# First layer of a two-layer kernel: the value product as seven half-size products, and the output product in another place of the period

## The chip, the cores and the metric

The kernel runs on one core of a Trainium2 chip. A core has a matrix engine (PE, TensorE), a vector engine (DVE), an activation engine (ACT), a general engine (POOL, GpSimd) and a queue that only issues transfers here (SP, SyncE). Each engine has its own stream of instructions and carries them out in program order; semaphores order the streams against one another. Tiles live in SBUF; matmul results go to PSUM, which has eight banks of 128 partitions x 512 fp32 values.

The metric is device time of one execution in microseconds (us). The kernel before takes 935.56 us, the median of three runs (935.55 to 936.3).

## The reference

Eight batches of 512 tokens with 256 features pass through two layers. In both, the layer's input is normalised and two branches are added to it.

```python
scores = einsum('bnqd,bnkd->bnqk', q, k) / sqrt(L)          # q, k: xn @ W + b, then RoPE; 16 heads of L=64
attn   = softmax(where(causal, scores, -1e9))
attended = einsum('bnqk,bnkd->bnqd', attn, v)               # v = xn @ Wv + bv
x = x + attended @ Wo + bo + quantised(xn)                  # int8 rounding of xn, product with int8 weights
xn = layernorm(x)
x = x + (mask * softmax(comparison)) @ xn + sigmoid(xr @ Wr.T) * (square(relu(xk @ Wk.T)) @ Wv2.T)
```

`RoPE` multiplies by cosines and sines, with the sines meeting the other member of each pair. The scale of the quantised branch is the greatest magnitude over all eight batches, so that branch can only begin when the last batch has been normalised. The second layer isn't touched by the change.

## The kernel before

All products of the attention are fp32. The first layer works on 16 groups, `at` = 0 to 15: group `at` is batch `b = at // 2` and half `g = at % 2` of its 16 heads, 8 heads each. The order of all instructions is written out by hand (`tc.manual_schedule()`); no planner decides it, and each engine's stream follows from the order of the calls. The loop at L842, `for at in range(1, last)` with `last = 15`, handles in one period several groups at different stages: it ends group `at-1`, does the softmax of group `at`, and projects for groups `at+1` and `at+2`.

The matrix engine's order in one period is: scores of run 0 (L509); the weighing product of group `at-1`, probabilities times values (`weigh`, L597); scores of run 1; the queries' product for group `at+1` (`project(at+1, 0)`, L428); scores of run 2; the values' product for group `at+1` (`project_v`, L472); scores of runs 3 and 4; the output product of group `at-1` (`finish`, which calls `output_product`, L390, and `add_output`, L399, for each half); the keys' product for group `at+2` (`project(at+2, 1)`, L428). The scores of a group are cut by query blocks into five runs (`RUNS`, L34), so that softmax on the other engines can follow run by run.

A `project` call for a group of 8 heads is two calls of `project_qk` (indices `2*at` and `2*at+1`, four heads each). In one, two products go into two banks; ACT moves each to a tile `l` with its bias (L434); four DMAs on SP copy `l` to a tile `y` with its quarters of partitions exchanged (L436). `turn_qk` then does the RoPE: DVE multiplies `h = l * cos` (`turn_own`, L446) and `y = y * sin` (`turn_other`, L446), and POOL adds them (`h = h + y`, L461). The `l` and `y` tiles have two buffers each.

`project_v` makes the values of a group in four banks, each from four matmuls of 512 columns (two per bank for each of the two halves of the 256 input features), which ACT copies to a tile `v` (L478); two DMAs store it to DRAM (`va<-v`, L479), and `load_v` fetches it in another layout (`vr<-va`, L489) after the next period's weighing.

`soften` is the lower part, in which DVE reads the scores from PSUM, adds the mask, scales and finds the row minimum of the negated scores (L537), and then the exponential on ACT, with its sum (L541). `divide` takes reciprocals on DVE (L552) and multiplies by them on POOL (L560). `turn` transposes the probabilities on DVE (L580). The probabilities lie in a pool, `prob`, with four buffers for each tag (a tag is a kind of tile).

The next batches' input is handled in the same loop: `look_at` (statistics), `prepare` (normalising, greatest magnitude), `turn_x` (DVE transposes in L325, SP stores the result with `xnf<-xs`, L329, and fetches it as `xnT` with four DMAs, `xnT<-xnf`, L188), and `load_x` for the batch after it (L81). `look_at` and `prepare` come in odd periods, `turn_x` and `load_x` in even ones from `at = 4`; batches up to 2 are turned on PE (`transpose_x`). SP takes all its transfers in program order, and waits at each for what it needs; the four fetches of `xnT` wait until the store of the same data has landed.

`add_biases` (L380) adds the output bias to a batch's result on POOL. In periods 12 and 13 the first two batches' quantised products are fitted in (`fetch_input`, `round_input`, `clip`, `add_quantised`). `bank` gives the eight banks of PSUM in rotation. A bank asked for again waits until its last reader is done.

## Time and profile before

| what | value |
|---|---|
| median of three runs | 935.56 us (935.55 to 936.3) |
| profiled execution, span | 934.3 us |
| profiled execution's own time | not listed apart; the median is 1.3 us above the span, for what lies around it |
| granted clock of the matrix engine | 1.00 in every period looked at |
| length of periods 7, 8, 9 and 10 (between starts of weighing) | 44.24, 44.51, 44.23, 45.70 us |
| length of periods 1, 12, 13, 14 | 45.50, 45.97, 44.92, 42.73 us |
| value product (L472), 256 matmuls in all | 114.3 us |
| output product (L390), 512 matmuls in all | 114.9 us |

The profile is of one execution. For each engine it lists busy time and idle time, and what ended the idle time (the releaser). Matmuls are pipelined, so the length of a single matmul says less than that of a run of equal ones: 16 of 512 columns are 7.06 us from first to next, 32 of 256 columns 7.10 us. The busy time that a group shows can be more than such a row gives for each instruction, as neighbours overlap. The chain of work is followed back from the last instruction, at each step to what released it. Tile names are `out<-in`; `sc` are scores, `pq` the queries' or keys' bank, `pv` the values' bank, `pw` the output product's bank, `av` the weighed values, `p` the probabilities, `t` their transposes.

### The profile page before, as it was taken

What the parts mean: (1) busy time and instruction counts of PE and PEld (TensorE: products, weight loads), DVE (VectorE), ACT (ScalarE), POOL (GpSimd) and SP (SyncE); (2) the same over time, 40 slices, a digit from 0 to 9 for tenths busy, and PEclk for the clock granted to TensorE, in tenths of its full rate; (3) what the DMA queues carried; (4) which work ended last, traced back from release to release, by engine and by line L of the source; (5) the groups of instructions that cost most, each with busy time, mean ns of one, the idle gap of its engine ahead of it and who ended that gap; (6) DMA issues with size and microseconds to landing.
All of it is one profiled execution on the core that took longest, in us unless ns stands there. A gap on an engine that the chain in (4) does not pass through costs nothing.

```text
span 934.3 us, 27432 instructions
## 1 busy us (share of the span) xinstructions
PE 919.8 (98%) x10451; PEld 594.7 (64%) x10451; DVE 793.3 (85%) x2441; ACT 528.3 (57%) x1478; POOL 542.2 (58%) x688
## 2 busy tenths in 40 slices
PE   9998999999999999999999999999999999999998
PEld 5446565656566575757565656566657777777776
DVE  4998898898899889988998899999899588888854
ACT  3585564647465646474746556555577444445553
POOL 2576766655665667566665756678667323444311
PEclk9999999999999999999999999999999999999999
DMA  7667354525543464245444635563435133221011
GB/s 213 194 165 213 102 138 130 121 75 132 169 105 97 109 182 132 75 115 172 123 95 114 179 93 145 151 154 97 110 108 127 47 102 79 74 50 48 25 33 34
DMA packets 70290, 108.03 MB, mean 116 GB/s; under 512 B 8592, under 2 KB 49040, under 8 KB 70160
## 3 DMA queue, kind: packets, MB, share of 16 engines
q1 hardware_dynamic: 68288, 104.64, 42.2%
q10 hardware_dynamic: 1872, 1.64, 0.7%
q8 instruction: 83, 1.36, 0.6%
q14 instruction: 47, 0.39, 0.1%
HBM read 41.76 MB, written 28.84 MB: 76 GB/s over the span
## 4 chain that ended last, share of the span: by engine, by line
PE 85%; DVE 6%; DMA 3%; issue 1%; POOL 1%; SPq 1%; ACT 1%; DVEq 0%; ACTq 0%; POOLq 0%
PE pq L428 21%; PE av L597 14%; PE sc L509 11%; PE pw L390 10%; PE pv L472 8%; PE po L756 6%; PE pk L703 3%; PE pg L718 3%; PE pvv L730 3%; DVE t L580 2%; PE c L675 2%; PE trc L743 1%; PE plr L245 1%; DVE p L537 1%; DMA xnl<-xnf 1%
## 5 line engine op out<-in xcount | busy, mean ns | idle before, releaser
L541 ACT ACTIVATE p<-p,nm 128x64 f32<-128x64 f32 (+15 forms) x512 | 260.0, 512 | 123.8 <-DVE nm L537 100.9
L560 POOL TENSOR_SCALAR p<-p,rs 128x512 f32<-128x512 f32 (+4 forms) x504 | 265.4, 547 | 44.6 <-DVE rs L552 42.6
L461 POOL TENSOR_TENSOR h<-h,y 128x1024 f32<-128x1024 f32 x62 | 161.1, 2598 | 181.5 <-DVE y L446 102.2
L537 DVE CUSTOM_DVE_ANT_0 p<-sc,cmask 128x64 f32<-128x64 f32 (+15 forms) x512 | 190.2, 434 | 53.7 <-PE sc L509 53.7
L580 DVE STREAM_TRANSPOSE t<-p 128x256 f32<-128x256 f32 (+3 forms) x640 | 192.2, 367 | 17.9 <-POOL p L560 17.8
L509 PE MATMUL sc<-h,h 64*32 64x512 f32 (+15 forms) x4096 | 138.7, 393 | 1.3 <-POOL h L461 1.2
L597 PE MATMUL av<-t,vr 32*64 32x384 f32 (+15 forms) x4096 | 128.8, 392 | 3.7 <-issue 3.7
L597 PEld LDWEIGHTS av<-t,vr 32*64 32x64 f32 x4096 | 122.8, 131 | 9.2 <-issue 7.9
L509 PEld LDWEIGHTS sc<-h,h 64*32 64x32 f32 x4096 | 78.6, 106 | 78.5 <-issue 58.3
L434 ACT ACTIVATE l<-pq,cs 128x512 f32<-128x512 f32 x128 | 84.7, 683 | 67.6 <-PE pq L428 53.3
L390 PE MATMUL pw<-wo,att 128*128 128x256 f32 x512 | 114.9, 382 | 0.8 <-DVE nm L537 0.8
L446 DVE TENSOR_TENSOR y<-y,cs 128x1024 f32<-128x1024 f32 x64 | 110.6, 1728 | 5.1 <-DMA y<-l 5.1
L428 PE MATMUL pq<-xnT,wq 128*128 128x512 f32 x256 | 114.6, 599 | 0.2 <-ACT xnT L349 0.2
L428 PE MATMUL pq<-xnT,wk 128*128 128x512 f32 x256 | 113.1, 593 | 1.4 <-DVE x L399 1.0
L472 PE MATMUL pv<-wv,xnT 128*128 128x512 f32 x256 | 114.3, 599 | 0.0
L390 PEld LDWEIGHTS pw<-wo,att 128*128 128x128 f32 x512 | 95.9, 190 | 19.5 <-issue 6.1
L541 ACT ACTIVATION_READ_ACCUMULATOR p<-p,nm 128x1 f32 x512 | 97.3, 190 | 0.0
L428 PEld LDWEIGHTS pq<-xnT,wk 128*128 128x128 f32 x256 | 48.3, 190 | 58.2 <-issue 55.4
L472 PEld LDWEIGHTS pv<-wv,xnT 128*128 128x128 f32 x256 | 47.3, 190 | 57.9 <-issue 54.5
L446 DVE TENSOR_TENSOR h<-l,cs 128x1024 f32<-128x1024 f32 x64 | 80.0, 1252 | 4.3 <-ACT l L434 4.3
L428 PEld LDWEIGHTS pq<-xnT,wq 128*128 128x128 f32 x256 | 47.2, 190 | 56.0 <-issue 48.8
L611 ACT ACTIVATE att<-av,cs 128x512 f32<-128x512 f32 x64 | 38.7, 688 | 71.3 <-PE av L597 71.3
(114 smaller groups left out, 940.7 us busy)
## 6 DMA issues: line engine op xcount, KB each, us to landing
y<-l SPq DMA_DIRECT2D x256, 128.0 KB, 2.3
va<-v SPq DMA_DIRECT2D x32, 512.0 KB, 3.1
vr<-va SPq DMA_DIRECT2D x64, 256.0 KB, 5.1
x<-in_x SPq DMA_DIRECT2D x15, 512.0 KB, 5.0
x1f<-x SPq DMA_DIRECT2D x7, 512.0 KB, 3.2
out<-y SPq DMA_DIRECT2D x14, 256.0 KB, 2.2
xnf<-xs SPq DMA_DIRECT2D x5, 512.0 KB, 3.6
xnT<-xnf SPq DMA_DIRECT2D x20, 128.0 KB, 2.8
```

The costliest lines, as they stand in the source:

```text
L390: nc.tensor.matmul(pw[:, j, :], atts[at, p][:, tok], wo[:, 4 * (at % NH) + p, :], start=(p == 0), stop=(p == 3),)
L428: nc.tensor.matmul(pb.rearrange("p (t a r) -> p t a r", a=4, r=Q), w[:, g, k, bass.ts(t, P)], xnT[b][:, k].rearrange("p a (t r) -> p t a r ...
L434: nc.scalar.activation(l[:, t, :], pb, AF.Identity, bias=cs[:, bias : bias + 1])
L446: nc.vector.tensor_tensor(dst, src, table[:, None, :].to_broadcast([P, 2, S]), ALU.mult)
L461: (engine or nc.gpsimd).tensor_tensor(h, h, y, ALU.add)
L472: nc.tensor.matmul(pb.rearrange("p (g n) -> p g n", g=2), xnT[b][:, k, 2 * half + j], wqkv[2][:, 2 * g : 2 * g + 2, k, :], start=(k == 0), ...
L509: nc.tensor.matmul(scored[at, i][e][j * Q : j * Q + Q, :], q[rows, j % 2, bass.ts(i, Q)], k[rows, j % 2, :n], start=True, stop=True,)
L537: nc.vector.tensor_tensor_reduce(p[:, e, col : col + n], sc, cmask[:, S - n :], -1.0 / L**0.5, BIG, ALU.add, ALU.min, nm[:, c : c + 1],)
L541: nc.scalar.activation(p[:, e, col : col + n], p[:, e, col : col + n], AF.Exp, bias=nm[:, c : c + 1], scale=-1.0, accum_out=sm[:, c : c + 1],)
L560: nc.gpsimd.tensor_scalar(p, p, rs[:, c : c + 1], 1.0, ALU.mult, ALU.mult)
L580: nc.vector.transpose(turned[at][c][:, :, at_ : at_ + (n - 1) * pitch(c) + 1 : pitch(c), :], p[:, :, c * P : c * P + n * Q].rearrange("p e ...
L597: nc.tensor.matmul(banks[j][e * L : e * L + L, i * Q :], vs[at][rows, c, m, bass.ts(e, L)], t[c][rows, e, m * pitch(c) + m : m * pitch(c) ...
```

## The change

The value product of groups 2 to 15 is made by `project_v_by_seven`. The product is seen as two by two blocks: the 256 input features in two halves, the token tiles in two halves on one side, and the weight columns of the group in two halves on the other. With sums and differences of blocks (the Winograd form of Strassen's scheme) seven block products give what eight gave. Each is two matmuls of 256 columns, so 28 matmuls instead of 16 of 512. Four of them go to one bank, `x`, one after another: each adds to what is there, and ACT copies the bank after each (`keep`). One goes to bank `y` and two to bank `z`; DVE adds those banks to the kept copies (`add`), three times. The sums of weight blocks are made once, on POOL, at `at = 1` (`sum_weights`, four operations, which overwrite a block of `wv`); the differences of input blocks are made on POOL once for each batch, in odd periods (`mix_input`, four operations).

The order of the period changes with it. `finish(at-1)`, the output product, comes between runs 2 and 3 of the scores, where `project_v` was. `project_v_by_seven(at+1)` ends the period. The keys' product for the first four heads of `at+2` comes before it; that for the other four is cut in two, one bank after the second product into `x` and one after the third, by way of `amid`, which also holds the exponential and division of run 4 and the transposes of runs 3 and 4. `soften` is cut into `lower` and `raise_`. `turn_own` and `turn_other` of the second queries stand around the division of run 3.

`look_at(b+2)` comes before the scores of run 1 and `prepare(b+2)` before the division of run 1, instead of after the scores of run 1 and after the division of run 2. `turn_x(b+1)` and `load_x(b+2)` come before the division of run 1 and the queries' product in periods 4, 6, 8 and 10, instead of after the division of run 2; in period 12 `turn_x(7)` comes ahead of the division of run 2. In period 14 the seven products have nothing between them, and the loop is left after them.

The pool of probabilities has six buffers, and the program is built with `dynamic_dma_scratch_size=1024`.

```diff
--- before
+++ after
@@ -267,3 +267,3 @@
         qk = pool("qk", 4)
-        prob = pool("prob", 4)
+        prob = pool("prob", 6)
         attp = pool("att", 4)
@@ -383,6 +383,8 @@
 
-        def output_product(at, half):
+        def output_product(at, half, js=(0, 1)):
 
-            pw = bank(f"pw_{at}_{half}").rearrange("p (j n) -> p j n", j=2)
-            for j in range(2):
+            if 0 in js:
+                products[at, half] = bank(f"pw_{at}_{half}").rearrange("p (j n) -> p j n", j=2)
+            pw = products[at, half]
+            for j in js:
                 tok = bass.ts(2 * half + j, P)
@@ -393,3 +395,2 @@
                     )
-            products[at, half] = pw
 
@@ -414,3 +415,3 @@
 
-        def project_qk(at, which):
+        def project_qk(at, which, ts=(0, 1)):
 
@@ -420,7 +421,10 @@
 
-            l, y = (
-                prob.tile([P, 2, S], F32, tag="p", name=f"{tag}_{at}_{which}") if at == 1 else
-                work.tile([P, 2, S], F32, tag=tag, name=f"{tag}_{at}_{which}", bufs=2) for tag in "ly"
-            )
-            for t in range(2):
+            if 0 in ts:
+                evicted[at, which] = [
+                    prob.tile([P, 2, S], F32, tag="p", name=f"{tag}_{at}_{which}") if at == 1 else
+                    work.tile([P, 2, S], F32, tag=tag, name=f"{tag}_{at}_{which}", bufs=2)
+                    for tag in "ly"
+                ]
+            l, y = evicted[at, which]
+            for t in ts:
                 pb = bank(f"pq_{at}_{which}_{t}")
@@ -434,5 +438,5 @@
                 nc.scalar.activation(l[:, t, :], pb, AF.Identity, bias=cs[:, bias : bias + 1])
-            for n in range(4):
-                nc.sync.dma_start(y[bass.ts(n ^ 1, Q)], l[bass.ts(n, Q)])
-            evicted[at, which] = l, y
+            if 1 in ts:
+                for n in range(4):
+                    nc.sync.dma_start(y[bass.ts(n ^ 1, Q)], l[bass.ts(n, Q)])
 
@@ -483,2 +487,82 @@
 
+        wv = wqkv[2].rearrange("p (g h) k n -> p g h k n", h=2)
+        wv_sums = work.tile([P, 2, 3, 2 * P], F32, name="wv_sums")
+
+        def sum_weights():
+            one, two, three = (wv_sums[:, :, n] for n in range(3))
+            (a11, a12), (a21, a22) = ([wv[:, :, h, k] for k in range(NK)] for h in range(2))
+            for dst, x, y, op in (
+                (one, a21, a22, ALU.add), (two, one, a11, ALU.subtract),
+                (a21, a11, a21, ALU.subtract), (three, a12, two, ALU.subtract),
+            ):
+                nc.gpsimd.tensor_tensor(dst, x, y, op)
+
+        mixes = {}
+
+        def mix_input(b):
+            t = work.tile([P, 4, 2, P], F32, tag="tx", name=f"tx_{b}")
+            (b11, b12), (b21, b22) = ([xnT[b][:, k, 2 * h : 2 * h + 2] for h in range(2)] for k in range(NK))
+            for dst, x, y in ((0, b12, b11), (1, b22, t[:, 0]), (2, b22, b12), (3, b21, t[:, 1])):
+                nc.gpsimd.tensor_tensor(t[:, dst], x, y, ALU.subtract)
+            mixes[b] = t
+
+        def project_v_by_seven(at, amid={}):
+            b, g = divmod(at, NH)
+            stores[at] = away.tile([4, P, NT * P], F32, tag="v", name=f"va_{at}")
+            s1, s2, s4 = (wv_sums[:, g, n] for n in range(3))
+            (a11, a12), (s3, a22) = ([wv[:, g, h, k] for k in range(NK)] for h in range(2))
+            t1, t2, t3, t4 = (mixes[b][:, n] for n in range(4))
+            b11, b21, b22 = xnT[b][:, 0, 0:2], xnT[b][:, 1, 0:2], xnT[b][:, 1, 2:4]
+            x, y, z = (bank(f"pv_{at}_{n}").rearrange("p (j n) -> p j n", j=2) for n in range(3))
+            v = [work.tile([P, 4, 2, P], F32, tag="v", name=f"v_{at}_{half}", bufs=2) for half in range(2)]
+
+            def product(to, left, right, fresh=False):
+                for j in range(2):
+                    nc.tensor.matmul(
+                        to[:, j, :], left[:, j], right, start=fresh and j == 0, stop=True,
+                        skip_group_check=j > 0 or not fresh,
+                    )
+
+            def part(half, g_):
+                return v[half][:, 2 * g_ : 2 * g_ + 2].rearrange("p r j n -> p j r n")
+
+            def of(bank_):
+                return bank_.rearrange("p j (r n) -> p j r n", r=2)
+
+            def keep(half, g_):
+                nc.scalar.copy(part(half, g_), of(x))
+
+            def add(bank_, half, g_):
+                nc.vector.tensor_tensor(part(half, g_), of(bank_), part(half, g_), ALU.add)
+
+            def store(half):
+                nc.sync.dma_start(
+                    stores[at][:, :, half * 2 * P : half * 2 * P + 2 * P].rearrange("r p n -> p r n"),
+                    v[half].rearrange("p r t n -> p r (t n)"),
+                )
+
+            def then(step):
+                amid.get(step, lambda: None)()
+
+            product(x, b11, a11, True)
+            keep(0, 0)
+            then(0)
+            product(y, b21, a12, True)
+            product(z, t1, s1, True)
+            product(x, t2, s2)
+            keep(1, 0)
+            add(y, 0, 0)
+            then(1)
+            product(x, t3, s3)
+            keep(1, 1)
+            then(2)
+            add(z, 1, 1)
+            product(x, t4, a22)
+            keep(0, 1)
+            store(0)
+            then(3)
+            product(z, b22, s4)
+            add(z, 1, 0)
+            store(1)
+
         def load_v(at):
@@ -516,2 +600,6 @@
         def soften(at, run):
+            lower(at, run)
+            raise_(at, run)
+
+        def lower(at, run):
 
@@ -540,7 +628,15 @@
                         )
+                    col += n
+
+        def raise_(at, run):
+            nm, sm = sums_of[at][:2]
+            for us in RUNS[run]:
+                for i in us:
+                    for e in range(2):
+                        p = chances[at, i][:, e, :]
+                        c = 2 * PLACE[i] + e
                         nc.scalar.activation(
-                            p[:, e, col : col + n], p[:, e, col : col + n], AF.Exp,
-                            bias=nm[:, c : c + 1], scale=-1.0, accum_out=sm[:, c : c + 1],
+                            p, p, AF.Exp, bias=nm[:, c : c + 1], scale=-1.0,
+                            accum_out=sm[:, c : c + 1],
                         )
-                    col += n
 
@@ -567,3 +663,3 @@
 
-        def turn(at, run):
+        def turn(at, run, units=slice(None)):
 
@@ -574,3 +670,3 @@
                 ]
-            for i in (i for us in RUNS[run] for i in us):
+            for i in (i for us in RUNS[run][units] for i in us):
                 p = chances.pop((at, i))
@@ -847,3 +943,4 @@
             scores(at, 0)
-            turn(at - 1, 4)
+            if at == 1:
+                turn(at - 1, 4)
             soften(at, 0)
@@ -865,2 +962,4 @@
             turn_qk(2 * at + 3, 1)
+            if g == 1 and 1 <= b < B - 2:
+                look_at(b + 2)
             if at == last - 2:
@@ -876,3 +975,6 @@
             elif g == 1 and 1 <= b < B - 2:
-                look_at(b + 2)
+                prepare(b + 2)
+            if g == 0 and 1 < b < B - 2:
+                turn_x(b + 1)
+                x_next.append(load_x(b + 2))
             divide(at, 1)
@@ -881,2 +983,6 @@
             project(at + 1, 0)
+            if at == 1:
+                sum_weights()
+            if g == 1:
+                mix_input(b + 1)
             if at in (last - 3, last - 2):
@@ -890,2 +996,4 @@
                 clip(xnl, xq)
+            if at == last - 3:
+                turn_x(b + 1)
             divide(at, 2)
@@ -893,8 +1001,2 @@
                 prepare(2)
-            elif g == 1 and 1 <= b < B - 2:
-                prepare(b + 2)
-            if g == 0 and 1 < b < B - 1:
-                turn_x(b + 1)
-                if b + 2 < B:
-                    x_next.append(load_x(b + 2))
             if at == last - 1:
@@ -904,5 +1006,6 @@
                 add_biases(0)
-            project_v(at + 1)
             if at == last - 1:
+                project_v_by_seven(at + 1)
                 break
+            finish(at - 1)
             if at == 2:
@@ -911,8 +1014,6 @@
             scores(at, 3)
-            soften(at, 3)
-            turn_qk(2 * at + 3, 0)
-            turn(at, 2)
-            divide(at, 3)
+            lower(at, 3)
+            raise_(at, 3)
             scores(at, 4)
-            soften(at, 4)
+            lower(at, 4)
             if at in (last - 3, last - 2):
@@ -920,7 +1021,24 @@
                     add_quantised(s_, half, xq, line(f"u_{s_}_{half}"))
-            finish(at - 1)
-            turn(at, 3)
-            if two:
-                project(at + 2, 1)
-            divide(at, 4)
+            turn_own(2 * at + 3, 0)
+            divide(at, 3)
+            turn_other(2 * at + 3, 0)
+            project_qk(2 * at + 4, 1)
+            turn(at, 2)
+
+            def step_one():
+                raise_(at, 4)
+                divide(at, 4)
+
+            def step_two():
+                turn(at, 3, slice(0, 1))
+                project_qk(2 * at + 5, 1, (0,))
+
+            def step_last():
+                turn(at, 3, slice(1, 2))
+                turn(at, 4)
+
+            project_v_by_seven(
+                at + 1,
+                {0: step_one, 1: step_two, 2: lambda: project_qk(2 * at + 5, 1, (1,)), 3: step_last},
+            )
             if g == 0 and b < B - 1:
@@ -1096,3 +1214,5 @@
 
-    nc = bacc.Bacc("TRN2", target_bir_lowering=False, num_devices=1)
+    nc = bacc.Bacc(
+        "TRN2", target_bir_lowering=False, num_devices=1, dynamic_dma_scratch_size=1024
+    )
     arrays, args = {}, []
```

## The prediction, made before the result was known

> **What bounds the kernel now.** I read the busy times and the chain of work that ended last first.
>
> ```profile
> PE 919.8 (98%) x10451; PEld 594.7 (64%) x10451; DVE 793.3 (85%) x2441; ACT 528.3 (57%) x1478; POOL 542.2 (58%) x688
> ...
> PE 85%; DVE 6%; DMA 3%; issue 1%; POOL 1%; SPq 1%; ACT 1%; DVEq 0%; ACTq 0%; POOLq 0%
> PE pq L428 21%; PE av L597 14%; PE sc L509 11%; PE pw L390 10%; PE pv L472 8%; PE po L756 6%; PE pk L703 3%; PE pg L718 3%; PE pvv L730 3%; DVE t L580 2%; PE c L675 2%; PE trc L743 1%; PE plr L245 1%; DVE p L537 1%; DMA xnl<-xnf 1%
> ```
>
> TensorE (PE) is the bound, at 98% of the span; the value product (pv, L472) is 8% of the chain. So work taken off PE is time won, if the others keep up. VectorE (DVE), at 85%, is next. I cut the span at the starts of the weighing products (L597): one stretch is one period. Columns: stretch and length; then busy time and instructions of PE, weight loads, DVE, ACT, POOL; clock, DMA share, GB/s. The rows are periods 7, 8 and 10.
>
> ```profile
> 344.82:389.06 44.24, 44.24 (x595) 27.69 (x597) 41.15 (x138) 26.17 (x80) 27.62 (x37) 1.00 0.38 97
> 389.06:433.57 44.51, 44.51 (x595) 27.75 (x597) 37.77 (x128) 26.40 (x80) 29.14 (x40) 1.00 0.56 156
> 477.80:523.50 45.70, 45.01 (x595) 27.58 (x597) 37.76 (x128) 26.40 (x80) 29.12 (x40) 1.00 0.57 151
> ```
>
> PE is full in both kinds of period; an odd one leaves DVE 3.1 us free, an even one 6.7. Then period 8 engine by engine: PE, SyncE's queue (SP, which issues the DMAs in program order), DVE (start, length, line, tile).
>
> ```profile
> 399.25 7.13 PE L428 MATMUL pq<-xnT,wq 128*128 128x512 f32 x16
> 406.32 2.01 PE L509 MATMUL sc<-h,h 64*32 64x384 f32 x64
> 408.26 7.13 PE L472 MATMUL pv<-wv,xnT 128*128 128x512 f32 x16
> ...
> 417.64 7.17 PE L390 MATMUL pw<-wo,att 128*128 128x256 f32 x32
> ```
> ```profile
> 404.54 6.09 SPq L436 DMA_DIRECT2D y<-l  x8
> 416.72 0.35 SPq L329 DMA_DIRECT2D xnf<-xs  x1
> 419.37 2.08 SPq L188 DMA_DIRECT2D xnT<-xnf  x4
> 421.50 0.43 SPq L81 DMA_DIRECT2D x<-in_x  x1
> ```
> ```profile
> 403.97 0.20 DVE L552 RECIPROCAL rs<-sm 128x4 f32<-128x4 f32 x2
> ...
> 411.40 1.22 DVE L446 TENSOR_TENSOR y<-y,cs 128x1024 f32<-128x1024 f32 x1
> ```
>
> The thing to see: the eight y<-l copies that RoPE needs are issued before the next input is stored and turned (xnf<-xs, xnT<-xnf), and y is multiplied 7 us after their issue began. The chain of period 10 shows how long the turning holds the queue, since the fetches wait for the store to land:
>
> ```profile
> 504.84 1.20 DVE xs L325 x2
> ...
> 506.06 3.93 DMA xnf<-xs
> ...
> 511.30 3.07 DMA xnT<-xnf
> ```
>
> The sum is made against the profiled span, 934.3 us; 1.3 us lie around it, to the median of 935.56.
>
> **Seven products for eight (at=1 to 14).** The old product is 16 matmuls of 512 columns in 7.06 us, 441 ns each. The new one is 28 of 256 columns. The nearest row is pw: 32 of 256 columns in 7.10 us, 222 ns each. 28 x 0.222 = 6.21 us, a gain of 0.85 per period on PE, and 14 x 0.85 = 11.9 us at most. If a half-size matmul cost 252 ns nothing would be won; no row speaks for that. The Trainium skill, page "TensorE: Matmul & The Clock Gate", section "Back-to-back issue gap", speaks against the change: spacing is set by weight load and matmul together, 81 ns at 128 columns and 131 at 512, so by its line (an estimate from that page, some 0.75 of the time for half the columns) 28 would take 9.3 us and the sum would be some 43 us higher. The trace does not agree with that line: the pw row shows 0.50.
>
> It adds three DVE additions (PSUM and SBUF to SBUF; like add_output, L399, 0.6 us each, 1.8 per period), four tensor operations of 128x256 on POOL in odd periods (add_biases is the same form: 4 x 0.70 and gaps, 2.9), and four of 128x512 at at=1 (twice the columns, 4 x 1.2 = 4.8). The ACT copies stay four. In odd periods DVE has 3.1 us free for 1.8; in even ones 6.7.
>
> **Even periods 4, 6, 8, 10: turning the input goes ahead of the y copies.** On period 8's times: transposes of run 0 end at 403.97, the xs transposes 1.2 later, 405.2. SP then holds store, its landing, four fetches and the x load, 506.06 to 512.21 in period 10, 6.15 us, so is free at 411.35. Four y<-l issues took 2.45 us and their landing 2.28: y is there at 416.1. DVE comes to it at 411.4 as before, so it stands 4.7 us. Behind y stand on DVE: ten transposes (2.76), two reciprocals, both additions of the output product (1.2, which free its banks), the lower part of run 3 (to 421.3). Exp of run 3 follows on ACT to 426.0, two evictions 1.3 and the first kept copy 0.55: 427.85. PE, which has no other work in order, reaches the fourth product (it writes the bank just copied) at 417.7 + 3.53 keys + 3 x 0.89 = 423.9. PE loses 3.95. Per period -0.85 + 3.95 = +3.1. In period 4 an old y wait goes (-1.05) and the spreading of weights stays (+0.8): +2.85; in period 10 the old wait for xnT (0.35 net) goes: +2.75. Sum 3.1 x 2 + 2.85 + 2.75 = +11.8. From below: if the turning took no queue time, -0.85 and the two old waits, -4.0 in all; from above, no slack at all, +0.75 each.
>
> **Odd periods 3 to 11.** look_at and prepare (1.75 and 2.5 us of DVE) move ahead of the reciprocals of run 1, so divide 1 starts on POOL 2.25 us later. In before, a POOL add and a DVE multiply that meet both stretch:
>
> ```profile
> 349.14 3.34 POOL L461 TENSOR_TENSOR h<-h,y 128x1024 f32<-128x1024 f32 x1 [4.96 <-DVE rs L552]
> ...
> 350.19 3.38 DVE L446 TENSOR_TENSOR y<-y,cs 128x1024 f32<-128x1024 f32 x1
> ```
>
> (2.36 and 1.22 when alone.) With mix_input behind divide 1, divide 2 starts at 374.65 instead of 371.1 (period 7). From there POOL has h 2.36, divide 3.65, about 2.3 of such meetings, divide 3.65, h 2.36, divide 0.93; the last transposes of run 4 end at 388.35 and weighing can start at 388.95, against 389.06 before. The gain is eaten: 0 each. Ends: -0.85 where the meetings don't happen, +1.0 where they come twice.
>
> **Single periods.** at=1: POOL has sum_weights 4.8, mix 2.9 and the bias work 3.5 ahead of divide 3 and of the keys' h. These fill its idle 5.6 us and push h to 119.9, the last transposes to 121.5, weighing from 118.0 to 122.1: +4.1 (ends -0.85 and +4.1 + 1). at=2: the output product now covers the wait for the turned x: -0.7. at=12: the keys of the last batch need xnT of batch 7, whose fetches end on SP at 601.2 and land 2.8 later, 604.0. PE had come there at 605.04, after the output product; now it comes at 597.1 and stands 6.9: 604.0 + 3.53 keys + 6.21 products + 3.53 keys + 1.88 scores = 619.15 against 613.96, +5.2 (below -0.85, if the turning is as early as it is in program order). at=13: mix beside rounding and the quantised additions on POOL and DVE: +1.3 (-0.85 to +3). at=14: the seven products have no other work between them. Each of x's waits for its copy (0.8), and the last waits for a DVE addition queued behind turn and RoPE work that ends at 687.2: scores of run 3 at 689.4 instead of 684.88, less what is won back: +2.45 (-0.9 to +4.7).
>
> **Other edits.** Six probability buffers and the split of soften remove waits that I cannot find in the groups (idle before L537 is for PE's scores): 0, with up to -0.5 a period if exp of run 4, now behind the first kept copy, had been held by a buffer; nothing above 0, as the split only delays exp by one copy of 0.55 us under the first products. The output product between runs 2 and 3 covers divide 2 as the value product did, by the same 7.1 us; without that cover, scores of run 3 would still go on, but the transposes of run 2 would come 3.65 later, behind the keys' 3.5 us. Its x1f store on SP (0.34 us, even periods) comes earlier with it and stands behind the x load, ahead of the va stores, which come some 10 us later than now: vr, which they feed, is fetched after the next weighing, 19 us after the old stores (422.03 to 441.67), and weighed a period later still, so 0; with that cover gone, the 5.1 us landing of vr would show. The scratch size changes no instruction.
>
> **Sum.** 11.8 + 0 + 4.1 - 0.7 + 5.2 + 1.3 + 2.45 = +24.15: 935.56 + 24.15 = 959.7 us. Its own range: all lower ends but the queue's give -4.25 (odd), -4.95, -2.15, -3.35, so 945; the upper ones +5, +1.7, +2.25, +3, so 971.
>
> **Rivals.**
> A, the queue costs nothing: y arrives in time, because the turning starts earlier than I place it or SP is free sooner; even periods give -4.0 in place of +11.8: 943.9 us. For it: the queue has 7 us between issue and use today; against it: 6.15 + 2.45 + 2.28 from 405.2.
> B, other side: PE stays the bound. All added work falls into the 6.7 and 3.1 us that DVE has free and POOL's 16; 935.56 - 11.9 - 1.4 (the old waits of periods 4 and 10) = 922.3 us. It decides at y's landing: up to 411.4 + 0.75 us the stall stays hidden, and the same must hold for at=1 and 12, where buffers could lend the slack. For it: the engine shares of the page. Against it: the in-order queues.
> C, the half-size products don't win (252 ns each): +11.9 on the forecast, 971.6 us. With it go odd periods that lose 1 to 1.5 us more each, 965 to 967 us, so together 965 to 972.
> D, no change: gains and new waits balance within 0.2%, about what a measurement of this kernel tells from no change (1.9 us).
>
> **How the numbers follow.** Forecast 0.62, A 0.13, C 0.07, B 0.15, D 0.03. Faster 0.15, same 0.03, slower 0.82. The predicted time is the forecast's. For the range, 971 above takes in the forecast's upper bound and half of C; below, 940 takes in all of A; left out are B, D and a little of C.
>
> **What the profile after would show.** Periods 4, 6, 8, 10 of 47 to 48 us, with DVE idle 4 to 5 us before the second RoPE multiply, released by y<-l, and the y<-l issues behind xnT<-xnf and x on SP; period 7 near 44.2; period 12 with PE waiting about 7 us for xnT<-xnf before the keys; period 1 with weighing at 122; value products of 222 ns each. I am wrong if even periods shrink to 43.7, if the y<-l issues keep their place, or if the products take over 250 ns.

## The result and the profile after

The changed kernel takes 989.01 us (median of four runs, 983.07 to 991.35) against 935.9 us: a ratio of 1.0556, with a 95% interval of 1.0521 to 1.0591. The forecast of 959.7 us had the sign and the place of the loss, but the time lies outside the range of 940 to 971. The profiled execution took 991.35 us, the longest of the four, with a span of 989.5 us and a mean granted clock of 0.974; the kernel before ran at 1.000 in its profile.

First the page of the changed kernel: busy times, then the two groups that changed most. The last two lines are the same groups of the kernel before.

```profile
PE 930.3 (94%) x10619; PEld 632.1 (64%) x10619; DVE 822.9 (83%) x2483; ACT 529.5 (54%) x1478; POOL 593.9 (60%) x720
...
L432 PE MATMUL pq<-xnT,wk 128*128 128x512 f32 x256 | 131.5, 653 | 34.6 <-DVE x L400 29.0
...
L450 DVE TENSOR_TENSOR y<-y,cs 128x1024 f32<-128x1024 f32 x64 | 112.3, 1754 | 30.9 <-DMA y<-l 30.8
```
```profile
L446 DVE TENSOR_TENSOR y<-y,cs 128x1024 f32<-128x1024 f32 x64 | 110.6, 1728 | 5.1 <-DMA y<-l 5.1
L428 PE MATMUL pq<-xnT,wk 128*128 128x512 f32 x256 | 113.1, 593 | 1.4 <-DVE x L399 1.0
```

PE's busy time rose by 10.5 us although it was given less to do: the same keys' product (pq with wk) is busy 131.5 us instead of 113.1, for which the cuts below show a slower clock. PE now stands 34.6 us before that product, against 1.4, and 29.0 of them were released by x, the addition of the output product on DVE. DVE in turn stands 30.8 us for y<-l, against 5.1.

The stretches of the changed kernel, cut at the starts of weighing, columns as in the prediction, show where it lies. The rows are periods 1, 7, 8, 10, 12, 13 and 14.

```profile
72.23:128.52 56.29, 46.82 (x604) 31.20 (x604) 38.47 (x130) 26.50 (x80) 40.75 (x49) 0.91 0.42 105
...
368.25:412.10 43.85, 43.85 (x619) 29.86 (x604) 42.48 (x139) 26.27 (x80) 34.13 (x41) 1.00 0.39 97
412.10:463.57 51.47, 45.85 (x620) 30.56 (x604) 40.20 (x131) 26.40 (x80) 30.18 (x40) 0.93 0.48 134
...
507.71:561.60 53.89, 48.40 (x621) 31.65 (x605) 40.03 (x131) 26.60 (x80) 30.15 (x40) 0.90 0.46 129
...
605.97:658.64 52.67, 46.16 (x613) 31.19 (x612) 45.19 (x140) 26.57 (x80) 34.70 (x43) 0.94 0.53 140
658.64:706.40 47.76, 45.34 (x629) 29.93 (x613) 44.96 (x140) 26.38 (x80) 37.65 (x44) 1.00 0.45 110
706.40:754.46 48.06, 42.85 (x675) 29.35 (x661) 42.22 (x143) 29.59 (x93) 28.66 (x36) 0.96 0.42 111
```

The clock stands at 1.00 in period 7, and below it in just those periods that grew long, but for 13. Period by period, the difference of the two profiled spans (55.2 us) is made up of these rows, and of 0.3 us less ahead of period 1:

| periods | before | after | difference | forecast |
|---|---|---|---|---|
| 4, 6, 8, 10 | 181.3 | 210.6 | +29.3 | +11.8 |
| 1 | 45.5 | 56.3 | +10.8 | +4.1 |
| 12 | 46.0 | 52.7 | +6.7 | +5.2 |
| 14 and the piece behind it | 71.1 | 78.7 | +7.7 | +2.45 |
| 13 | 44.9 | 47.8 | +2.8 | +1.3 |
| 3, 5, 7, 9, 11 | 221.4 | 220.6 | -0.9 | 0 |
| 2 | 47.2 | 46.3 | -0.9 | -0.7 |

Where the forecast named a sign, it came so; the sizes did not. The even periods 4, 6, 8 and 10 took 46.1, 45.0, 44.5 and 45.7 us before and take 52.7, 52.6, 51.5 and 53.9 now. Period 8 of the changed kernel, engine by engine as before: SP, DVE, PE (start, length, line, tile, and in brackets the idle time and its releaser).

```profile
428.93 0.34 SPq L329 DMA_DIRECT2D xnf<-xs  x1
431.57 1.73 SPq L188 DMA_DIRECT2D xnT<-xnf  x4
433.34 0.43 SPq L81 DMA_DIRECT2D x<-in_x  x1
433.88 6.34 SPq L441 DMA_DIRECT2D y<-l  x8
```
```profile
441.94 1.23 DVE L450 TENSOR_TENSOR y<-y,cs 128x1024 f32<-128x1024 f32 x1 [6.70 <-DMA y<-l]
...
445.96 1.26 DVE L400 TENSOR_TENSOR x<-pw,x 128x512 f32<-128x512 f32 x2
```
```profile
432.01 7.17 PE L392 MATMUL pw<-wo,att 128*128 128x256 f32 x32
439.12 2.39 PE L593 MATMUL sc<-h,h 64*32 64x320 f32 x80
446.68 5.60 PE L432 MATMUL pq<-xnT,wk 128*128 128x512 f32 x8 [5.17 <-DVE x L400]
```

The y copies come behind the turning and the load of x, as read from the program. The output product fills two of the eight banks, the scores of run 3 four and those of run 4 the other two; the keys' product then needs banks that DVE must first empty (the addition x<-pw), and DVE is waiting for y. Eight keys' matmuls then take 5.60 us, where a row of eight without a wait takes 3.70. The chain of that period has the pieces in order of time.

```profile
435.71 6.11 DMA y<-l
...
446.05 0.59 DVE x L400
```

The new thing is the 6.11 us from the end of the issue to the landing of y<-l; the row that I used for it said 2.28. And cutting the period just there (stretch, then engines and clock) shows the clock falling with PE's wait:

```profile
439.12:446.68 7.56, 2.39 (x81) 1.47 (x81) 4.74 (x15) 0.00 (x0) 2.94 (x3) 0.80 0.29 71
446.68:452.12 5.44, 5.44 (x8) 2.42 (x9) 5.44 (x25) 4.40 (x17) 3.22 (x8) 0.64 0.24 96
452.12:463.50 11.38, 11.38 (x85) 7.41 (x83) 9.89 (x29) 5.61 (x12) 10.58 (x15) 1.00 0.30 69
```

It is 0.64 through the eight keys' matmuls and 1.00 behind them: 1.9 us (5.60 against 3.70) that no wait shows.

### The profile page after: what moved, and what is told of

Its sections match the earlier page's. It is cut to its first block, busy times and chain, and to the rows that moved or that the text cites. A ratio compares the mean times of both kernels' runs of the same rounds, so it can differ in the third digit from the quotient of the medians.

```text
span 989.5 us, 27871 instructions
## 1 busy us (share of the span) xinstructions
PE 930.3 (94%) x10619; PEld 632.1 (64%) x10619; DVE 822.9 (83%) x2483; ACT 529.5 (54%) x1478; POOL 593.9 (60%) x720
## 4 chain that ended last, share of the span: by engine, by line
PE 70%; DVE 12%; DMA 6%; POOL 3%; issue 3%; SPq 3%; ACT 1%; DVEq 0%; POOLq 0%; ACTq 0%
PE pq L432 15%; PE av L693 13%; PE sc L593 8%; PE pv L521 8%; PE pw L392 6%; PE po L852 6%; DVE t L676 4%; DMA y<-l 4%; PE pk L799 3%; PE pg L814 3%; PE pvv L826 3%; DVE p L625 2%; DVE y L450 2%; PE c L771 2%; POOL p L656 2%
## 5 line engine op out<-in xcount | busy, mean ns | idle before, releaser
L656 POOL TENSOR_SCALAR p<-p,rs 128x512 f32<-128x512 f32 (+4 forms) x504 | 286.3, 589 | 78.2 <-DVE rs L648 77.9
L432 PE MATMUL pq<-xnT,wk 128*128 128x512 f32 x256 | 131.5, 653 | 34.6 <-DVE x L400 29.0
L693 PE MATMUL av<-t,vr 32*64 32x448 f32 (+15 forms) x4096 | 133.0, 393 | 7.3 <-issue 7.2
L450 DVE TENSOR_TENSOR y<-y,cs 128x1024 f32<-128x1024 f32 x64 | 112.3, 1754 | 30.9 <-DMA y<-l 30.8
L432 PEld LDWEIGHTS pq<-xnT,wk 128*128 128x128 f32 x256 | 52.6, 211 | 92.0 <-issue 50.7
L450 DVE TENSOR_TENSOR h<-l,cs 128x1024 f32<-128x1024 f32 x64 | 82.0, 1283 | 4.3 <-ACT l L438 4.3
L784 ACT ACTIVATE e<-c,nb 128x512 f32<-128x512 f32 x32 | 21.7, 684 | 72.6 <-DVE nb L779 72.0
L804 POOL TENSOR_TENSOR kk<-kk 128x512 f32<-128x512 f32 x16 | 18.5, 1180 | 51.7 <-ACT kk L803 51.7
```

Source lines behind the costliest of these rows:

```text
L432: nc.tensor.matmul(pb.rearrange("p (t a r) -> p t a r", a=4, r=Q), w[:, g, k, bass.ts(t, P)], xnT[b][:, k].rearrange("p a (t r) -> p t a r ...
L450: nc.vector.tensor_tensor(dst, src, table[:, None, :].to_broadcast([P, 2, S]), ALU.mult)
L656: nc.gpsimd.tensor_scalar(p, p, rs[:, c : c + 1], 1.0, ALU.mult, ALU.mult)
L693: nc.tensor.matmul(banks[j][e * L : e * L + L, i * Q :], vs[at][rows, c, m, bass.ts(e, L)], t[c][rows, e, m * pitch(c) + m : m * pitch(c) ...
```

## Experiments: the queue, the load of x, the order, and period 1

Four kernels, each the changed one with one edit.

**The load of x behind the y copies.**

```diff
                 turn_x(b + 1)
-                x_next.append(load_x(b + 2))
             divide(at, 1)
             ...
             project(at + 1, 0)
+            if g == 0 and 1 < b < B - 2:
+                x_next.append(load_x(b + 2))
```

> The changed kernel, with only the 512 KB load of x moved: in periods 4, 6, 8 and 10 SP issues it behind the eight y<-l copies of the queries instead of ahead of them. Theory (the y copies landed in 6.1 us instead of 2.3 because the load of x was in the transfer engines ahead of them): they land in 2.3 to 3 us, y comes 3.5 to 4 us earlier, PE's wait before the keys in period 8 falls from 5.2 to 1.3 to 1.7 us, and the wait being short the clock stays at 1.00 (another 2.1 us); even periods of 46 to 47 us, 988 - 4 x 5.5 = 962 to 970. Rival (the landing is long because of xnT's four fetches, or of the queue alone): 0.5 us of issue saved for each of four periods, 985 to 989.

Measured: 969.67 us, 1.0354 of the kernel before (1.0336 to 1.0371), at the upper end of the 962 to 970 expected; the first theory held in the main. Period 8 of this kernel, SP, DVE and PE:

```profile
423.85 1.73 SPq L188 DMA_DIRECT2D xnT<-xnf  x4
425.69 5.59 SPq L441 DMA_DIRECT2D y<-l  x8
431.32 0.58 SPq L81 DMA_DIRECT2D x<-in_x  x1
```
```profile
431.10 1.22 DVE L450 TENSOR_TENSOR y<-y,cs 128x1024 f32<-128x1024 f32 x1 [3.46 <-DMA y<-l]
```
```profile
435.84 3.70 PE L432 MATMUL pq<-xnT,wk 128*128 128x512 f32 x8 [1.93 <-DVE x L400]
```

PE's wait is 1.93 us instead of 5.17, and the eight keys' matmuls are back at 3.70. DVE stands 3.46 us for y instead of 6.70. The eight y copies take 3.2 to 3.8 us from issue to landing here, with the fetches of xnT still just ahead, and 2.3 to 2.5 in period 8 of the next run, with nothing just ahead: so the fetches have a part in the long landing, as the rival had it, and the load of x the larger one. The even periods are 47.1 to 48.2 us (46 to 47 expected), near the 47 to 48 of the forecast. So the load of 512 KB ahead of the y copies and the clock behind the longer wait are what the forecast of the even periods lacked, together 20 us of them (210.6 to 190.7).

**The turning at the start of the even periods**, and the load of x behind the y copies.

```diff
             soften(at, 0)
+            if g == 0 and 1 < b < B - 2:
+                turn_x(b + 1)
             ...
-            if g == 0 and 1 < b < B - 2:
-                turn_x(b + 1)
-                x_next.append(load_x(b + 2))
             divide(at, 1)
             ...
             project(at + 1, 0)
+            if g == 0 and 1 < b < B - 2:
+                x_next.append(load_x(b + 2))
```

> The changed kernel, with the turning of the input (xs transposes, store, four fetches) moved to the start of periods 4, 6, 8 and 10, behind the lower part of run 0, and the load of x behind the queries' y copies. Theory (the place of these transfers on SP's queue makes the whole loss of the even periods): even periods of 43.4 to 44.5 us instead of 51.5 to 53.9, period 1 and 12 to 14 unchanged; 988 - 4 x 8.2 = 953 to 958, with no DVE idle before y over 1 us in those periods. Rival (what is added to DVE and POOL makes part of the loss, or the turning hurts in its new place as well, by holding up vr or the keys' RoPE): even periods keep 2 us or more over 44, 964 or more.

Measured: 959.02 us (1.0242; 1.022 to 1.0263), a touch above the 953 to 958 expected. The even periods sum to 182.5 us against 210.6; DVE's idle time before y fell from 30.8 to 5.6 us, with none in these periods. Periods 4 and 8 are at 44.4 and 44.9 us, but 6 and 10 stay at 45.7 and 47.4, where PE stands 1.3 and 2.0 us in or just behind the weighing, for no releaser that the profile shows. In all four the fetches of xnT stand 4.6 to 6.3 us for their store, and vr behind them, so that this alone doesn't set 6 and 10 apart; in a later run, where the fetches come behind vr, the four take 43.6 to 44.0. Place on the queue makes all but a small part of the loss of the even periods.

**Eight products in the changed order.**

```diff
-            if at == 1:
-                sum_weights()
-            if g == 1:
-                mix_input(b + 1)
             ...
-            project_v_by_seven(
-                at + 1,
+            project_v(
+                at + 1, (0, 1),
                 {0: step_one, 1: step_two, ...
```

`project_v` takes the work in between as well, and makes the product of period 14 too.

> The changed kernel's order of work and buffers, with the value product by eight full products again (16 matmuls of 512 columns in the same place, the same work amid them), no sums of weights, no differences of inputs, no additions. Theory (the order loses, the seven products win 1.0 us a period on PE, as 28 x 0.2155 against 7.06): even periods stay at 52 to 54 us, odd ones grow by about 0.5 to 1.0 us to 44.5 to 45.2, period 1 falls by some 7 us as POOL loses 9.9 us of work; 986 to 998. Rival (the seven products' additions, copies and POOL work cause the loss): even periods go back to 44 to 46 us, 940 to 955.

Measured: 978.82 us (1.0454; 1.0438 to 1.0469). The order alone, without any of the seven products' work, loses 43 us. Its even periods are 51.0 to 51.6 us, as long as with seven. But the whole is 10 us faster than seven products (the changed kernel's own runs lie 8 us apart), where I had expected 986 to 998: the seven products lost on balance in this order. Periods 14 and 15 are here as in the kernel before (42.7 and 28.3 against 48.1 and 30.7). And period 1 is still 54.5 us, although POOL lost its 9.9 us of new work and I had expected some 7 us less, so I had its cause wrong.

**POOL's order in period 1.**

```diff
             scores(at, 0)
             if at == 1:
+                sum_weights()
                 turn(at - 1, 4)
             ...
             project(at + 1, 0)
             if at == 1:
-                sum_weights()
-            if g == 1:
+                nc.gpsimd.tensor_tensor(bob, bob, rw[:, 2, :], ALU.add)
+                add_biases(0)
+            if g == 1 and at > 1:
                 mix_input(b + 1)
             ...
             divide(at, 2)
             if at == 1:
-                nc.gpsimd.tensor_tensor(bob, bob, rw[:, 2, :], ALU.add)
-                add_biases(0)
+                mix_input(b + 1)
```

> The changed kernel with POOL's work of period 1 in another order: the sums of weights at the start of the period, where POOL stood idle, the biases of batch 0 ahead of the division of run 2, the differences of inputs behind it. Theory (period 1 loses 10.8 us because the addition of the output product waits on DVE for the biases, which stand on POOL behind 9.9 us of the new work, and PE for its banks): the addition comes 6 us or more earlier, PE's wait before the keys falls from 8.9 to under 2 us, period 1 from 56.3 to 45 to 48 us, so 977 to 981. Rival (the wait in period 1 has another last cause, as the fetch of the result's tile or y): 985 or more.

Measured: 975.68 us (1.0422; 1.0405 to 1.0439), a little under the 977 to 981 expected, with period 1 at 46.5 us instead of 56.3 and no wait of PE before its keys' product that reaches 0.5 us. The chain of period 1 in the changed kernel shows what was removed:

```profile
94.85 2.24 POOL wv L498
97.09 2.22 POOL wv_sums L498
...
104.50 3.65 POOL p L656 x8
...
108.91 1.41 POOL x L380 x2
...
110.34 0.70 DVE x L400
...
111.09 6.14 PE pq L432 x8
```

The addition of the output product (x L400) needs the biases that POOL adds (x L380), and they stood behind the division of run 2. In the kernel before this addition came after the scores of run 4; the change put it in front, ahead of what it depends on. PE waited 8.86 us with the new work on POOL and 5.71 without, and both times the eight keys' matmuls behind the wait took over 6 us. The run moves three things at once on POOL, and which of them gave how much it doesn't tell.

## Experiments: one part alone, all waits away, and the seven products' worth

**The moved turning alone, on the kernel before.** Only the place of `turn_x` and `load_x` in periods 4, 6, 8 and 10 is taken from the change.

```diff
+            if g == 0 and 1 < b < B - 2:
+                turn_x(b + 1)
+                x_next.append(load_x(b + 2))
             divide(at, 1)
             ...
             divide(at, 2)
             ...
-            if g == 0 and 1 < b < B - 1:
+            if at == last - 3:
                 turn_x(b + 1)
-                if b + 2 < B:
-                    x_next.append(load_x(b + 2))
```

> The kernel before with one part of the change alone: in periods 4, 6, 8 and 10 the turning of the input and the load of x stand ahead of the division of run 1 and the queries' product, and so ahead of the queries' y copies on SP. Theory (the place on the queue delays y whatever the value product is; here 7 us of value product lie between the scores of runs 2 and 3, so PE feels less): y is there 6 to 7 us late, DVE idle before y 20 us or more in all, even periods 46 to 49 us, 943 to 952. Rival (in the old order the slack behind the scores covers the late y): DVE idle as large, but even periods of 44 to 45.5 us, 933 to 938.

Measured: 949.75 us (1.0135; 1.0114 to 1.0155), and DVE idle before y as long as in the changed kernel:

```profile
L446 DVE TENSOR_TENSOR y<-y,cs 128x1024 f32<-128x1024 f32 x64 | 109.8, 1716 | 34.7 <-DMA y<-l 34.1
```

The theory held: even periods of 46.6 to 48.4 us. Three periods that the edit doesn't touch, 1, 2 and 5, took another 5.3 us together, at a clock of 0.96 to 0.97. The same stall of DVE costs the even periods only 9.8 us in the old order (191.1 against 181.3), but 24 to 29 in the new: 29.3 in the changed kernel, 24.2 in the run that changes period 1 alone, and 23.9 with eight products. In the old order the value product, whose banks ACT empties, lies between the scores of runs 2 and 3, and the output product only follows behind run 4. So the loss has two parts: the queue makes DVE late, and the new order of PE's work makes PE feel it at once. That it is the place of the output product in that order is read from the waits before the keys; no run moved it alone.

**All waits found taken away together**, with the seven products.

```diff
             soften(at, 0)
+            if g == 0 and 1 < b < B - 1:
+                turn_x(b + 1)
             ...
             load_v(at)
+            if g == 0 and 1 < b < B - 1:
+                fetch_turned(b + 1)
             ...
             project(at + 1, 0)
+            if g == 0 and 1 < b < B - 1:
+                fetch(b)
+            if g == 0 and 1 < b < B - 2:
+                x_next.append(load_x(b + 2))
             ...
-                project_v_by_seven(at + 1)
+                project_v_by_seven(at + 1, {0: one, 1: two_, 2: three})
```

`turn_x` now ends with the store, and `fetch_turned` has its four fetches. Period 1 is as in the run with POOL's order changed, `fetch(b)` moves from the start of the period, and in period 13 `mix_input` stands behind the division of run 2. In period 14, `one` holds the scores and the softening of run 3, `two_` and `three` a quarter of the output product each.

> All waits found so far taken away together, the seven products kept: the turning of the input stored at the start of the even periods 4 to 12 and fetched behind vr, the fetch of the result's tile and the load of x behind the queries' y copies, period 1 as in the run with its POOL order changed, the differences of inputs behind the division of run 2 in period 13, and in period 14 the scores of run 3 and the first half of the output product between the seven products. Theory (queue, bias and cover make all of the loss, and the seven products then give what PE saves): periods 4 to 11 of 43.3 to 44.5 us, 1 of 46.5, 12 of 44 to 46, 13 of 46 to 47, 14 of 42 to 44; 927 to 936, at or under the kernel before. Rival (DVE and POOL, with the new work, are now the bound): even periods over 45 us and 938 or more.

Measured: 943.45 us (1.0079; 1.0063 to 1.0096), above the 927 to 936 expected. Periods 4 to 11 came out as the theory had them, 43.6 to 44.5 us, and so DVE and POOL don't hold them above 45 us, as the rival had it. But periods 12 to 15 kept their loss: 48.1, 47.2, 50.8 and 30.9 us against 46.0, 44.9, 42.7 and 28.3. In period 12 no wait for xnT is left. My cover in period 14 was worse than none: the fifth product waited 4.8 us for ACT's copy, which stood behind the exponentials of run 3.

**The same order with eight products.** Its edit is that of the run with eight products above, made to the last run; the work that only the seven products need on POOL is gone.

> The same order as the run with all waits taken away, with the value product by eight full products and none of its sums, differences and additions. It prices the seven products alone, in an order where nothing else waits. Theory (they are worth what PE saves, 7.06 - 28 x 0.2155 = 1.03 us a period): 10 to 14 us slower than the seven products in the same order. Rival (their additions on DVE and sums on POOL eat the gain): within 4 us of it, or faster.

Measured: 936.91 us (1.0001; 0.9989 to 1.0013). It is 6.5 us faster than seven products in the same order, where the theory said 10 to 14 slower. The two profiles say why. In periods 4 to 11 the seven products win: those eight periods take 355.2 us with eight products and 351.0 with seven, 0.5 us a period. In periods 12 to 15 they lose 11.6 us. The price of the product can be read in the same period, 5, of either kernel. The profile shows two matmuls for each call of the program here: 8 calls are its 16 matmuls of 512 columns, and the two calls of each of the seven products, 14 in all, its 28 of 256. First with eight products, keys' matmuls between them:

```profile
286.34 3.60 PE L478 MATMUL pv<-wv,xnT 128*128 128x512 f32 x8
289.77 1.88 PE L434 MATMUL pq<-xnT,wk 128*128 128x512 f32 x4
291.49 1.88 PE L478 MATMUL pv<-wv,xnT 128*128 128x512 f32 x4
293.20 1.88 PE L434 MATMUL pq<-xnT,wk 128*128 128x512 f32 x4
294.92 1.88 PE L478 MATMUL pv<-wv,xnT 128*128 128x512 f32 x4
296.73 1.96 PE L598 MATMUL sc<-h,h 64*32 64x512 f32 x48
```

From start to next start that is 3.43 + 1.71 + 1.81 = 6.95 us. With seven, in the last kernel below:

```profile
284.36 1.89 PE L527 MATMUL pv<-wv,xnT 128*128 128x256 f32 x8
286.09 1.89 PE L527 MATMUL pv<-wv_sums,tx 128*128 128x256 f32 x8
287.81 1.88 PE L434 MATMUL pq<-xnT,wk 128*128 128x512 f32 x4
289.53 1.03 PE L527 MATMUL pv<-wv,tx 128*128 128x256 f32 x4
290.39 1.88 PE L434 MATMUL pq<-xnT,wk 128*128 128x512 f32 x4
292.11 1.03 PE L527 MATMUL pv<-wv,tx 128*128 128x256 f32 x4
292.97 1.03 PE L527 MATMUL pv<-wv_sums,xnT 128*128 128x256 f32 x4
293.93 1.96 PE L599 MATMUL sc<-h,h 64*32 64x512 f32 x48
```

That is 3.45 + 0.86 + 0.86 + 0.96 = 6.13 us, a gain of 0.82 where nothing waits; the forecast said 0.85.

**The differences of inputs later.** In periods 3 to 11, too, `mix_input` stands behind the division of run 2.

> The run with all waits taken away, with the differences of inputs behind the division of run 2 in periods 3 to 11 too, as it is in 1 and 13. Theory (POOL's chain through the odd periods, divide 1, differences, h, divide 2 to h and divide 4, ends just before weighing, so that it costs what the odd periods lack of the full gain of 1.03): odd periods fall from 43.5 to 44.3 us to 43.2 to 43.5, the whole by 1 to 4 us. Rival (odd periods are held by DVE, and POOL has slack): within 1 us of the other.

Measured: 947.6 us (1.0118; 1.0102 to 1.0134), 4 us slower than without. The odd periods are the same (220.0 us in all, both times), so POOL's chain doesn't hold them. The difference lies where the code is the same, in periods 1, 8 and 13 most of all and in 1.3 us ahead of period 1; I can't say why.

**Seven products up to period 11, then the old order.** Periods 12 to 14 are as in the kernel before. For that POOL restores the overwritten block of the weights.

```diff
+        def whole_weights():
+            (a11, _), (s3, _) = ([wv[:, :, h, k] for k in range(NK)] for h in range(2))
+            nc.gpsimd.tensor_tensor(s3, a11, s3, ALU.subtract)
             ...
+            old = at >= 12
             ...
             divide(at, 2)
+            if old:
+                if at == 12:
+                    whole_weights()
             ...
+                project_v(at + 1)
             ...
```

> Periods 1 to 11 as in the run with all waits taken away (seven products, early turning), periods 12 to 14 in the order of the kernel before with eight full products, for which POOL restores the overwritten block of the weights (one operation of 128x512, 1.3 us) in period 12. Theory (the seven products gain where nothing else is added, 0.4 us a period in 4 to 11, and lose only in 12 to 15): period 12 starts 7 us earlier than in the kernel before, 12 to 15 last as there (46.0, 44.9, 42.7, 28.3), so 927 to 931. Rival (the new order pushes its costs behind its last period): periods 12 to 15 keep 4 us or more of their loss, 932 or more.

Measured: 944.98 us (1.0094; 1.0079 to 1.0109), above the 927 to 931. Periods 13 to 15 take what they took before to 0.02 us, and period 12 starts 7.7 us earlier. But it lasts 60.5 us:

```profile
593.14 8.67 PE L478 MATMUL pv<-wv,xnT 128*128 128x512 f32 x16 [13.71 <-POOL wv L504]
```

PE waited for the one operation, of 1.26 us, that I had put behind the division of run 2, where the biases stand in period 1 of the changed kernel. The last run moves it alone:

```diff
             scores(at, 0)
             ...
+            if at == 12:
+                whole_weights()
             ...
             divide(at, 2)
-                if at == 12:
-                    whole_weights()
```

> The run with seven products up to period 11 and the old order behind it, with one operation moved: POOL restores the overwritten block of the weights at the start of period 12, where POOL stands idle, and not behind the division of run 2, where PE waited 13.7 us for it. Theory (that wait is all that period 12 lost): period 12 of 46 to 47 us instead of 60.5, the rest unchanged, 927 to 931, under the kernel before by 0.5 to 1%. Rival (the wait hid another, the x1 or xnl transfers or the clock): 933 or more.

Measured: 930.77 us against 937.29 (0.9925; 0.9909 to 0.994), and period 12 takes 46.7 us, so the theory held. This kernel is faster than the changed one, and than the kernel before by 0.75%, a small difference but clear of its interval. PE is 99% busy, and the clock holds.

```profile
PE 913.3 (99%) x10583; PEld 618.1 (67%) x10583; DVE 816.1 (88%) x2474; ACT 527.1 (57%) x1478; POOL 591.6 (64%) x717
...
PEclk9999999999999999999999999999999999999999
```

Not all of that gain is the seven products'. Periods 4 to 11 take 358.5 us in the kernel before, 355.2 with eight products in the order without the waits, and 351.4 here: 3.3 of the 7.1 us come with the order.

## Why the prediction was right in sign and wrong in size

The sum missed 31 of the 55 us: 17.5 in the even periods, 6.7 in period 1, 5.2 in period 14 and behind it, 1.5 each in 12 and 13, less 1.4 in the other rows. The steps that failed are, in the even periods, the landing of y (6.11 us, not 2.28) and the clock behind PE's waits (9.2 us in all, put at nothing), and in period 1 what PE waits for: the biases, 8.86 us, where the sum had only POOL's chain up to the keys. The upper end of its range left out the +1 of period 1 (972.7 with it); the measured time lies above that too.

**The gain.** 28 x 0.222 us by the row of the output product: right, 0.82 us measured against 0.85, and not the 9.3 us of the estimate beside it. Periods 4 to 11 net 0.5 of it in the same order with and without.

**Even periods: the mechanism right, one term mis-sized and one absent.** The forecast's step was "their landing 2.28", taken from a case in which nothing stood just ahead of the y copies. With four fetches and 512 KB of x ahead it was 6.11 us; the run that only moved x brought the wait on PE from 5.17 to 1.93 us. The term for the turning was too long the other way (6.15 us of queue forecast; 4.95 measured, from the store's issue at 428.93 to the first y issue at 433.88), and so was that for four issues (2.45 against some 1.8), so a part cancelled by luck: DVE stood 6.70 us for y, 4.7 forecast. PE's waits before the keys came to 20.2 us in the four periods, where the forecast had some 15.8 (3.95 each). The second term was absent, put at nothing: behind such a wait PE runs slower for a while. The eight keys' matmuls behind the four waits took 9.2 us more than 3.70 each, twice the error of the waits. The other 4 us of the miss lie elsewhere in these periods, among them waits of 1.1 and 1.7 us in the weighing of periods 4 and 10. The place of the wait was also another. I put it at the fourth product, waiting for a copy on ACT; it came earlier, at the keys, waiting for the banks of the output product, which I had named only in the clause that these banks are freed by the additions. By the forecast's own times the first of these additions ends some 3 us after PE comes to the keys, so the place alone hardly changes the sum.

**Period 1: right sign, wrong step.** "Push h to 119.9, the last transposes to 121.5" priced POOL's chain up to the keys' RoPE. The wait that decided was the addition of the output product waiting for `add_biases(0)`. I had listed that bias work on POOL, and knew that the output product was moved ahead, and did not join the two. The order alone gives 54.5 us there, without any new work on POOL, and with the biases earlier and the new work around them period 1 took 46.5. The sums of weights were also mis-sized, 7.1 us measured against 4.8, as two of the four operations took 2.2 us each instead of 1.3.

**Period 12**: xnT came as forecast (PE went on 36.3 us into the period, 36.1 forecast), though PE had come later, after a wait of 1.47 us for the banks of the output product, and so stood 5.04 us instead of 6.9. What was left out is the clock behind the wait: the eight keys' matmuls took 5.07 us, not 3.70. **Period 13**: PE stood 0.9, 0.6 and 0.7 us for DVE; +1.3 was too small. **Period 14**: the uncovered products wait 0.7 to 1.6 us each for ACT and DVE, 4.5 us in all, and the last four matmuls behind them take 2.07 us instead of 1.03. The mechanism was right, +2.45 too small. In two other runs with the same code there (turning early, POOL's order) the clock stayed at 1.00, and period 14 and the piece behind it cost 4.0 us instead of 7.7. **Odd periods**: 0 forecast, -0.2 on average; the gain was eaten there as said, but not by the place of `mix_input`.

**The rivals.** That the queue costs nothing (944) and that PE stays the bound (922) fell with the even periods. That half-size products don't win fell with the 0.82 us. That gains and waits balance fell with the total. None of the rivals held the clock or the banks, and a forecast with one loss per period added up on an engine at 98% left out that waits there cost more than their length.

The clock can be read from the waits before the keys. After the four waits of 1.72 to 2.81 us in the even periods of the run with x moved the eight matmuls took 3.70 us each time. After waits of 3.82 to 8.86 us in the changed kernel they took 5.07 to 6.56. The longest of the first kind and the shortest of the second:

```profile
344.02 3.70 PE L432 MATMUL pq<-xnT,wk 128*128 128x512 f32 x8 [2.81 <-DVE x L400]
```
```profile
543.75 6.56 PE L432 MATMUL pq<-xnT,wk 128*128 128x512 f32 x8 [3.82 <-DVE x L400]
```

The Trainium skill, page "TensorE: Matmul & The Clock Gate", section "Why this matters for your kernels", says to leave no gaps above some 3 us between bursts of matmuls, as one idle window takes the clock down. These rows agree. The forecast summed the waits and did not apply this to them.

Shorter waits go both ways, though. The weighing of period 1 comes after a wait of 2.3 us in every kernel; here are the run with all waits taken away and the last kernel, whose code is the same there:

```profile
72.28 9.69 PE L695 MATMUL av<-t,vr 32*64 32x512 f32 x256 [2.31 <-issue]
```
```profile
72.36 8.05 PE L699 MATMUL av<-t,vr 32*64 32x512 f32 x256 [2.32 <-issue]
```

The clock is 0.79 in the first 8 us of the one and 1.00 in the other. So the length of a wait alone doesn't decide, and this accounts for most of what periods 1 and 5 lost in the run that moved the turning alone: there the weighing took 9.65 us behind a wait of 2.33 and 9.68 behind one of 3.00 us, while behind another of 3.00, in period 9, it took 8.04.

What stays open: the changed kernel's runs spread over 8 us, those of the kernel before beside them over 1 (over up to 4 in the later comparisons). The clock's part behind equal waits differs from period to period (1.9 us behind 5.17 in period 8, 2.9 behind 3.82 in period 10); and the even periods, in the run that changes period 1 alone, came to 205.5 us instead of 210.6 with the same code; what decides it no run here shows. A difference of some 5 us between two kernels that both have such waits can be this alone. Whether six probability buffers matter by themselves wasn't measured: every run in the new order kept them.

## What to carry to other kernels

Where one engine is at 98%, price a new wait on it with what follows: in the changed kernel each wait of over 3.8 us before the keys cost 1.4 to 2.9 us more in clock. A step that is moved forward takes its inputs' due times with it: list for each moved addition or fetch who makes its inputs and where that stands on its own queue (the biases of period 1 and my own restored weights each cost PE 9 to 14 us for about 1 to 4 us of POOL work). A landing time from a row holds for what stood ahead of that transfer there; with four fetches and a load of half a megabyte ahead, 2.3 us became 6.1.

## What the runs showed that was not expected

The order that the change chose costs 43 us with eight products; with the turning, two loads and one POOL step put elsewhere, and the scores of run 3 amid the products of period 14, it costs nothing (0.9989 to 1.0013). So the loss of periods 4 to 11 lay in no engine's amount of work: DVE and POOL had 30 and 52 us more busy time in the changed kernel, and with the waits away these periods are still 4.2 us shorter with seven products than with eight. In periods 12 to 15 the seven products lost 11.6 us even so. Also, nearly equal stalls of DVE (34.1 and 30.8 us in all) cost the even periods 9.8 us in one order of PE's work and 24 to 29 in the other.
